# Mixed bands of the first convolution one band later, the upper parts of plain bands copied on ScalarE

## The chip, the cores and the metric

One core of a Trainium2 chip. The metric is the device time of one execution in microseconds (us); a kernel's time is the median of its runs. The profile of one execution shows the engines TensorE (PE, with its weight loads as PEld), VectorE (DVE), ScalarE (ACT), GpSimd (POOL) and SyncE (SP, which issues transfers).

## The reference

The input x is 4 images of 128 channels, 64 by 64, in fp32. Two layers follow each other:

```python
# layer 0: attention over the 4096 positions of an image, 4 heads of 32
x = x + proj(softmax(q @ k.T * scale) @ v)        # q, k, v from a group norm of x
# layer 1: two 3x3 convolutions with quantized weights
out = conv3x3(x, lsq_quantize(w1, alpha1))
out = relu(batchnorm(out, gamma1, beta1))
out = conv3x3(out, lsq_quantize(w2, alpha2))
out = relu(batchnorm(out, gamma2, beta2) + x)
```

The batch norms take mean and variance over all images and positions of a channel. So the first convolution must be complete before the second can start, and the second before the output. The change lies in the two convolutions, which are called the first and the second layer below.

## The kernel before, in words

The order of the instructions on each engine is written out by hand: what the Python code emits first for an engine stands first in its queue. Attention takes up to about 2233 us of the span. It writes its result to `y0` in device memory, and the convolutions read it from there.

A convolution works in 16 bands of 16 rows, four to an image (`bandlist`; band m is image m // 4, rows 16 * (m % 4) on). A band is loaded with a row of margin on each side as a tile `t` of 128 x 18 x 66 (1188 elements a partition). Its fp32 values are split into an upper part, written in the type fp32r, and a lower part, the rest, also in fp32r; both are multiplied by the same weights.

**A plain band** (`split` at L570, `conv` at L803) has `hi`, a copy of `t` (L573), and `lo = t - hi` (L574). TensorE does 9 taps x 2 parts x 2 halves = 36 matmuls of 512 columns (L810) into a PSUM tile of two banks. Each half is then read by VectorE for the statistics (`bn_stats`, L924) and by ScalarE, which copies it to `cv` (L925).

**A mixed band** (`mixed` at L585, `conv_by_two` at L849, `rows_of_two` at L860) computes two rows at a time from sums and differences of rows, with two thirds of the matmuls. VectorE makes `vo` (L591) and the two halves of `vi` (L593, L594); ScalarE copies them to the upper parts `uo` and `ui` (L602); VectorE subtracts for the lower parts `lo` and `li` (L604). TensorE does 24 matmuls (L856) with mixed weights `wmix` (made by `mix_weights`, L840) and the outer taps, into four banks: two in `a`, two in `c`. ScalarE copies one result (L864), VectorE combines all four with four operations (L865 to L868) and takes two statistics (L915).

Which bands are mixed is `BY_TWO` (L583), a set for each layer. PSUM has three two-bank buffers (`pss`, tag "s") and two one-bank buffers (`psa`, tag "a"). The `a` of a mixed band is a `pss` buffer; its `c` is in turn another `pss` buffer or both `psa` buffers (L905). The last band, 15, is plain and uses the two `psa` buffers, one for each half. The band tiles share nine SBUF buffers in `kpool`; the lower parts and `ui` of mixed bands have six more, `upper`.

`layer` (L895) goes over the bands: first band m's matmuls, then `prepare(m)`, which readies band m + 2, then the reading of band m's results. In the first layer `prepare` is `first` (L949): it issues the load of band m + 3 (`load_band`, L608), and splits band m + 2 (`split_band`, L613). It also does three things at fixed bands: `count_bad` (a count that decides at the end whether a general version runs: two small VectorE operations, `big` and `bad`, a matmul `nbad` into a `psa` buffer, and a VectorE copy to `cnt`), the load of the second layer's weights `raw_w` and their copy to `wq[1]`, and `mix_weights(1)` at band 14. Bands 0 and 1 are split while attention ends, and their matmuls and the split of band 2 are interleaved with its last block.

In the second layer `prepare` is `second`, which calls `relu_band` (L977). For a plain band it calls `relu_rows` (L966): ScalarE writes `t` as Relu of the normalized `cv` (L970), then come `hi` (L973) and `lo` (L974). For a mixed band ScalarE's Relu is L981. The first band of the second layer has its own code (L999, L1002).

Of the kernel before, what the change touches and what calls it, by code (L numbers as in the profile page):

```python
# [78 lines left out]
def _fast_body(ctx, tc, x, norm_w, norm_b, qkv_wt, qkv_b, proj_wt, proj_b,  # L79
               w1, alpha1, gamma1, beta1, w2, alpha2, gamma2, beta2, out, cnt):  # L80
    nc = tc.nc
# [142 lines left out]
    def stack_tile(name):  # L224
        return kpool.tile([P, KW], F32R, name=name, tag="k")

    def f32(t):
        return t.bitcast(F32)
# [77 lines left out]
    def keep_warm(count):  # L306

        t = psa.tile([P, FB], F32, name=f"idle{count}", tag="a")
        for _ in range(count):
            nc.tensor.matmul(t[:, 0:P], gavg, gavg, start=True, stop=True)  # L310
# [244 lines left out]
    def band_tile(name):  # L555
        return stack_tile(name).rearrange("p (r w) -> p r w", w=PW)
# [10 lines left out]
        lo, hi = max(r0, 0), min(r1, H)  # L567
        return f32(t)[:, lo - r0 : hi - r0, 1 : 1 + W], lo, hi

    def split(t, name):  # L570

        hi, lo = band_tile(f"hi{name}"), band_tile(f"lo{name}")
        nc.vector.tensor_copy(hi, f32(t))  # L573
        nc.vector.tensor_tensor(lo, f32(t), f32(hi), ALU.subtract)  # L574
        return hi, lo

    raw, ready = {}, {}
    bandlist = [(b, g) for b in range(B) for g in range(H // BR)]
# [1 line left out]

    BY_TWO = (set((3, 5, 7, 9, 11, 13)), set((2, 4, 6, 8, 10, 12, 14)))  # L583

    def mixed(t, name):  # L585

# [24 lines left out]
        nc.sync.dma_start(out=inner, in_=y0[b].rearrange("p (h w) -> p h w", w=W)[:, lo:hi, :])  # L611

    def split_band(b, g):  # L613
        way = mixed if bandlist.index((b, g)) in BY_TWO[0] else split
        ready[0, b, g] = way(raw[b, g], f"0_{b}_{g}")


# [185 lines left out]
    def conv(parts, ps, j, w):  # L803
        hi, lo = parts
        r0 = j * RB
        n = 0
        for part in (hi, lo):
            for tap in range(TAPS):
                kh, kw = divmod(tap, 3)
                nc.tensor.matmul(ps.rearrange("p (r w) -> p r w", w=W), w[:, tap, :],  # L810
                                 part[:, r0 + kh : r0 + kh + RB, kw : kw + W],
                                 start=(n == 0), stop=(n == 2 * TAPS - 1))
                n += 1

    def conv_tile(i, b, g):
        return pss.tile([P, 2, FB], F32, name=f"c{i}_{b}_{g}", tag="s")
# [32 lines left out]
    def conv_by_two(parts, a, c, i):  # L849

        for m, ps, w in ((1, a[0], wmix[:, 0, :, :]), (2, a[1], wmix[:, 1, :, :]),
                         (0, c[0], wq[i][:, 0:3, :]), (3, c[1], wq[i][:, 6:9, :])):
            n = 0
            for part in parts:
                for kw in range(3):
                    nc.tensor.matmul(ps.rearrange("p (r w) -> p r w", w=W), w[:, kw, :],  # L856
                                     part[m][:, :, kw : kw + W], start=(n == 0), stop=(n == 5))
                    n += 1

    def rows_of_two(a, c, y):  # L860

        even, odd = (y.rearrange("p (r e w) -> p r e w", e=2, w=W)[:, :, e, :] for e in range(2))
        a0, a1, c0, c1 = (u.rearrange("p (r w) -> p r w", w=W) for u in (*a, *c))
        nc.scalar.copy(odd, a1)  # L864
        nc.vector.tensor_tensor(even, odd, a0, ALU.add)  # L865
        nc.vector.tensor_tensor(odd, a0, odd, ALU.subtract)
        nc.vector.tensor_tensor(even, even, c0, ALU.add)
        nc.vector.tensor_tensor(odd, odd, c1, ALU.subtract)  # L868
# [11 lines left out]
    def batch_norm(i, st):  # L880

        mv = small.tile([P, 2], F32, name=f"bmv{i}", tag="mv")
        nc.vector.bn_aggr(mv, st)
        r = small.tile([P, 1], F32, name=f"br{i}", tag="rs")
        nc.vector.tensor_scalar(r, mv[:, 1:2], a_q[i], EPS, ALU.mult, ALU.add)
        nc.gpsimd.tensor_tensor(r, r, mhalf, ALU.pow)
        na = small.tile([P, 1], F32, name=f"bn{i}", tag="dv")
        nc.vector.tensor_tensor(na, r, a_n[i], ALU.mult)
        c = small.tile([P, 1], F32, name=f"bc{i}", tag="gc")
        nc.vector.scalar_tensor_tensor(c, mv[:, 0:1], na, bn[i][1], ALU.mult, ALU.add)  # L890
        a = small.tile([P, 1], F32, name=f"ba{i}", tag="ga")
        nc.vector.tensor_tensor(a, r, a_g[i], ALU.mult)
        return a, c

    def layer(i, prepare, done):  # L895


        st = mid.tile([P, B * NB, 6], F32, name=f"st{i}")
        end = mid.tile([P, 15], F32, name=f"end{i}")
        nc.gpsimd.memset(end[:, 0:1], float((B * NB - 2) * FB))  # L900
        for m, (b, g) in enumerate(bandlist[:-1]):
            if m in BY_TWO[i]:
                a = conv_tile(i, b, g)
                a = [a[:, j, :] for j in range(2)]
                if sorted(BY_TWO[i]).index(m) % 2:  # L905
                    c = [psa.tile([P, FB], F32, name=f"c{i}_{b}_{g}{j}", tag="a") for j in "xy"]
                else:
                    c = pss.tile([P, 2, FB], F32, name=f"c{i}_{b}_{g}z", tag="s")
                    c = [c[:, j, :] for j in range(2)]
                conv_by_two(ready[i, b, g], a, c, i)  # L910
                prepare(m)
                y = cv[b][:, 2 * g * FB : (2 * g + 2) * FB]
                rows_of_two(a, c, y)
                for j in range(2):
                    nc.vector.bn_stats(st[:, b * NB + 2 * g + j, :], y[:, j * FB : (j + 1) * FB])  # L915
                continue
            ps = done[m] if m < len(done) else conv_tile(i, b, g)
            for j in range(2):
                if m >= len(done):
                    conv(ready[i, b, g], ps[:, j, :], j, wq[i])  # L920
            prepare(m)
            for j in range(2):
                c = 2 * g + j
                nc.vector.bn_stats(st[:, b * NB + c, :], ps[:, j, :])  # L924
                nc.scalar.copy(cv[b][:, c * FB : (c + 1) * FB], ps[:, j, :])  # L925
        nc.vector.bn_aggr(end[:, 1:3], st.rearrange("p j s -> p (j s)")[:, : 6 * B * NB - 12])
        nc.vector.tensor_scalar(end[:, 2:3], end[:, 2:3], float((B * NB - 2) * FB), None, ALU.mult)
        b, g = bandlist[-1]
        for j in range(2):
            ps = psa.tile([P, FB], F32, name=f"c{i}_last{j}", tag="a")  # L930
            conv(ready[i, b, g], ps, j, wq[i])
            c = 2 * g + j
            nc.vector.bn_stats(end[:, 3 + 6 * j : 9 + 6 * j], ps)
            nc.scalar.copy(cv[b][:, c * FB : (c + 1) * FB], ps)
        prepare(len(bandlist) - 1)
        keep_warm(10)
        return batch_norm(i, end)

    def count_bad():

        big = small.tile([P, 1], F32, name="big")
        nc.vector.tensor_reduce(big, worst, AX.X, ALU.max)
        bad = small.tile([P, 1], F32, name="bad")
        nc.vector.tensor_scalar(bad, big, LIMIT, None, ALU.is_gt)
        nbad = psa.tile([P, FB], F32, name="nbad", tag="a")
        nc.tensor.matmul(nbad[0:1, 0:1], bad, ones[:, 0:1], start=True, stop=True)
        nc.vector.tensor_copy(cnt, nbad[0:1, 0:1])

    def first(m):  # L949
        if m == 4:  # L950
            count_bad()
        if m == 5:
            raw["w"] = f32(stack_tile("raw_w"))[:, : TAPS * P].rearrange("p (t o) -> p t o", o=P)
            nc.sync.dma_start(out=raw["w"], in_=wqd)
        if m == 6:
            nc.vector.tensor_copy(wq[1], raw["w"])
        if m == 14:
            mix_weights(1)
        if 0 < m < len(bandlist) - 3:
            load_band(*bandlist[m + 3])  # L960
        if m + 2 < len(bandlist) and m > 0:
            split_band(*bandlist[m + 2])
# [3 lines left out]
    def relu_rows(b, g, t, r0, r1):  # L966

        inner, lo, hi = t["inner"]
        a, e = max(r0 + g * BR - 1, lo), min(r1 + g * BR - 1, hi)
        nc.scalar.activation(inner[:, a - lo : e - lo, :],  # L970
                             cv[b].rearrange("p (h w) -> p h w", w=W)[:, a:e, :], AF.Relu,
                             bias=c1, scale=a1)
        nc.vector.tensor_copy(t["hi"][:, r0:r1, :], f32(t["t"])[:, r0:r1, :])  # L973
        nc.vector.tensor_tensor(t["lo"][:, r0:r1, :], f32(t["t"])[:, r0:r1, :],  # L974
                                f32(t["hi"])[:, r0:r1, :], ALU.subtract)

    def relu_band(b, g, pieces=((0, BR + 2),)):  # L977
        if bandlist.index((b, g)) in BY_TWO[1]:
            t = band_tile(f"t1_{b}_{g}")
# [13 lines left out]
    t = {n: band_tile(f"{n}1_{b0}_{g0}") for n in ("t", "hi", "lo")}  # L993
# [503 lines left out]
```

## Time and profile before

| what | value |
|---|---|
| median of 3 runs | 2516.44 us (2516.35 to 2517.39) |
| profiled execution | 2515.98 us, its span 2514.1 us |
| TensorE busy in the span | 2472.6 us (98%) |
| VectorE, ScalarE, GpSimd busy | 2205.4, 2106.9, 283.1 us |

By stage, in us from the start of the span:

| stretch | us | PE busy | DVE busy | ACT busy |
|---|---|---|---|---|
| attention, 0 to 2233 | 2233 | 2224.4 | 1994.2 | 2009.8 |
| bands 0 to 2, 2233 to 2262 | 29 | 29.0 | 16.2 | 2.1 |
| bands 3 to 14, 2262 to 2354 | 92 | 88.3 | 78.0 | 24.4 |
| band 15 and statistics, 2354 to 2366 | 12 | 10.9 | 4.8 | 3.1 |
| second layer, 2366 to 2484 | 118 | 117.7 | 91.3 | 49.2 |
| output, 2484 to 2514.1 | 30.1 | 2.3 | 20.9 | 18.4 |

A line of the timeline has the start in us, the time taken in us, the engine, the line of the kernel, the operation, the tile written, "<-" and the tiles read, the shapes, and how many instructions are merged; in brackets stands the idle time before it and what ended that. In the groups, the two numbers after the bar are busy us in all and the mean of one in ns, and the next is the engine's idle time just before them. PEclk is the share of the full TensorE clock that was granted.

### The profile page before, as it was taken

Reading aid. Unit: us, or ns where it says so; the run is one execution under the profiler, and the core shown is the slowest. Engines: PE = TensorE matmul, PEld = TensorE weight load, DVE = VectorE, ACT = ScalarE, POOL = GpSimd, SP = SyncE. Lnnn points to the kernel's source line nnn. Section 1 sums busy time; section 2 is a strip of 40 time slices with the busy share of each in tenths; the row PEclk is TensorE's granted clock in tenths of the full one; section 3 lists DMA queues with packets and bytes.
Section 4 is the critical chain, followed back from the end, with each engine's and each line's share of the span. In section 5 each row is a group of like instructions: output and inputs, shape, how many; then the busy total and the mean of one; then the engine's idle time right before and its main releaser. Section 6 shows DMA issues by size and latency. Waiting matters only on the chain.

```text
span 2514.1 us, 64863 instructions
## 1 busy us (share of the span) xinstructions
PE 2472.6 (98%) x28552; PEld 1474.0 (59%) x28552; DVE 2205.4 (88%) x1501; ACT 2106.9 (84%) x2291; POOL 283.1 (11%) x461
## 2 busy tenths in 40 slices
PE   9999999999999999999999999999999999999995
PEld 6555555555555555555555555555555555567774
DVE  6899888899988988889988889879999999978687
ACT  5999888999988899999988999989999999952344
POOL 2111111111011111111111111110001000100000
PEclk9999999999999999999999999999999999999998
DMA  6877677788766676788757666797666666664304
GB/s 194 191 184 170 167 177 171 175 197 190 182 156 166 171 173 152 169 213 189 168 141 184 177 148 167 172 216 174 139 143 147 143 134 152 135 131 94 109 1 168
DMA packets 148953, 403.84 MB, mean 161 GB/s; under 512 B 59416, under 2 KB 60184, under 8 KB 120120
## 3 DMA queue, kind: packets, MB, share of 16 engines
q0 software_dynamic: 45840, 280.39, 48.8%
q1 hardware_dynamic: 100952, 113.60, 17.1%
q8 instruction: 226, 3.70, 0.6%
q10 hardware_dynamic: 1872, 5.64, 0.6%
q14 instruction: 63, 0.52, 0.1%
HBM read 107.48 MB, written 56.42 MB: 65 GB/s over the span
## 4 chain that ended last, share of the span: by engine, by line
PE 87%; DMA 4%; issue 4%; DVE 3%; ACT 1%; SPq 1%; ACTq 0%; POOL 0%; POOLq 0%; DVEq 0%
PE s L442 40%; PE acc L456 36%; PE c L810 4%; DMA rm<-p 2%; DVE r L471 1%; DMA rc<-rd 1%; PE l L488 1%; PE pk L317 1%; PE pq L317 1%; PE c L856 1%; PE pv L317 1%; PE po L317 1%; DMA q<-qd 1%; SPq L422 0%; PE c_2z L856 0%
## 5 line engine op out<-in xcount | busy, mean ns | idle before, releaser
L444 ACT ACTIVATE p<-s 128x1024 f32<-128x1024 f32 x2048 | 1950.6, 1032 | 200.1 <-PE s L442 154.2
L471 DVE TENSOR_TENSOR r<-r,p 128x2048 f32<-128x2048 f32 x768 | 1758.0, 2289 | 64.3 <-ACT p L444 13.9
L442 PE MATMUL s<-q,k 64*128 64x512 f32 x8192 | 1138.3, 409 | 1.1 <-ACT p L444 0.9
L456 PE MATMUL acc<-p,v 128*32 128x256 f32 x16384 | 1026.4, 383 | 0.0
L442 PEld LDWEIGHTS s<-q,k 64*128 64x128 f32 x8192 | 715.7, 184 | 409.2 <-issue 165.8
L456 PEld LDWEIGHTS acc<-p,v 128*32 128x32 f32 x16384 | 462.5, 109 | 483.6 <-issue 248.1
L466 POOL DMA_DIRECT2D rm<-p x160 | 139.6, 873 | 796.5 <-ACT p L444 591.1
L925 ACT COPY cv<-c 128x512 f32<-128x512 f32 x34 | 20.0, 587 | 130.3 <-DVE st L924 130.3
L352 DVE SCALAR_TENSOR_TENSOR kst<-pk,b,kst 128x512 fp32r<-128x512 f32 x32 | 24.0, 750 | 83.5 <-PE s L442 68.5
L469 DVE TENSOR_TENSOR r<-p,p 128x2048 f32<-128x2048 f32 x32 | 73.2, 2288 | 11.1 <-ACT p L444 11.0
L810 PE MATMUL c<-hi,wq 128*128 128x512 f32 x306 | 79.1, 402 | 2.1 <-ACT hi L999 1.4
L810 PE MATMUL c<-lo,wq 128*128 128x512 f32 x306 | 78.5, 400 | 0.0
L352 DVE SCALAR_TENSOR_TENSOR qst<-pq,b,qst 128x512 fp32r<-128x512 f32 x32 | 24.0, 751 | 58.3 <-PE s L442 47.3
L810 PEld LDWEIGHTS c<-hi,wq 128*128 128x128 f32 x306 | 57.2, 188 | 19.7 <-issue 3.6
L810 PEld LDWEIGHTS c<-lo,wq 128*128 128x128 f32 x306 | 57.6, 188 | 15.4
L356 POOL DMA_DIRECT2D qd<-qst x31 | 23.6, 762 | 267.0 <-DVE qst L352 223.0
L492 POOL DMA_DIRECT2D r<-rm x31 | 26.2, 845 | 219.0 <-DMA rm<-p 87.5
L924 DVE BATCH_NORM_STATS2 st<-c 128x6 f32<-128x512 f32 x34 | 23.7, 696 | 20.0 <-ACT cv L925 11.2
L356 POOL DMA_DIRECT2D kd<-kst x27 | 20.0, 742 | 178.1 <-DVE kst L352 169.4
L488 PE MATMUL l<-r,ones 128*32 128x256 f32 (+1 forms) x504 | 37.7, 382 | 0.0
L351 ACT ACTIVATE kst<-pk,b 128x512 fp32r<-128x512 f32 x32 | 22.3, 700 | 18.3 <-PE pk L317 18.3
L464 POOL DMA_DIRECT2D rm<-p x32 | 17.9, 559 | 175.1 <-ACT p L444 84.3
(200 smaller groups left out, 1022.4 us busy)
## 6 DMA issues: line engine op xcount, KB each, us to landing
rm<-p POOLq DMA_DIRECT2D x192, 1024.0 KB, 7.9
q<-qd SPq DMA_DIRECT2D x248, 128.0 KB
r<-rm POOLq DMA_DIRECT2D x31, 1024.0 KB, 7.6
x<-in_x_dram SPq DMA_DIRECT2D x86, 256.0 KB
k<-kd SPq DMA_DIRECT2D x124, 128.0 KB
qd<-qst POOLq DMA_DIRECT2D x31, 512.0 KB, 5.2
kd<-kst POOLq DMA_DIRECT2D x27, 512.0 KB, 4.8
y<-x POOLq DMA_DIRECT2D x32, 256.0 KB, 6.4
```

Of the source, the lines that this page charges most:

```text
L317: nc.tensor.matmul(out[cs, :], w[:, cs], x, start=True, stop=True)
L352: nc.vector.scalar_tensor_tensor(lo, ps[what], bias, t[:, 0, :], ALU.add, ALU.subtract)
L356: (nc.sync if start else nc.gpsimd).dma_start(out=dst[b, j].rearrange("s p n -> p s n"), in_=t)
L442: nc.tensor.matmul(s[:, i, :], k[r, half, c0 : c0 + P], q[r, half, part, :], start=(part == 0), stop=(part == 1))
L444: nc.scalar.activation(pts[step][:, 2 * half : 2 * half + 2, :], s, AF.Exp, scale=SCALE)
L456: nc.tensor.matmul(acc[n][h * D : (h + 1) * D, cs], v[:, kt % KB, h * D : (h + 1) * D], pt[:, h, cs], start=(kt == 0 and half == 0), stop= ...
L466: nc.gpsimd.dma_start(out=msum[n], in_=pt, accum_op=ALU.add)
L469: nc.vector.tensor_tensor(rsum[n], pts[step - 1], pt, ALU.add)
L471: nc.vector.tensor_tensor(rsum[n], rsum[n], pt, ALU.add)
L488: nc.tensor.matmul(t["l"][h * D : (h + 1) * D, cs], ones, r[:, h, cs], start=first, stop=end)
L492: nc.gpsimd.dma_start(out=rsum[n], in_=msum[n], accum_op=ALU.add)
L810: nc.tensor.matmul(ps.rearrange("p (r w) -> p r w", w=W), w[:, tap, :], part[:, r0 + kh : r0 + kh + RB, kw : kw + W], start=(n == 0), stop ...
```

## The change

The mixed bands of the first layer move from 3, 5, ..., 13 to 4, 6, ..., 14; there are six of them still. In the first layer the upper part `hi` of the plain bands from 3 on is copied by ScalarE in place of VectorE; the second layer's `relu_rows` does the same. The choice of PSUM buffers for a mixed band's `c` is counted back from the last mixed band, which gets a `pss` buffer: in the first layer bands 14, 10 and 6 have `pss`, bands 12, 8 and 4 the two `psa` buffers; in the second layer each band keeps what it had. `count_bad` moves from band 4 to band 5.

```diff
-    def split(t, name):
+    def split(t, name, beside=True):
 
         hi, lo = band_tile(f"hi{name}"), band_tile(f"lo{name}")
-        nc.vector.tensor_copy(hi, f32(t))
+        if beside:
+            nc.vector.tensor_copy(hi, f32(t))
+        else:
+            nc.scalar.copy(hi, f32(t))
         nc.vector.tensor_tensor(lo, f32(t), f32(hi), ALU.subtract)
         return hi, lo
...
-    BY_TWO = (set((3, 5, 7, 9, 11, 13)), set((2, 4, 6, 8, 10, 12, 14)))
+    BY_TWO = (set((4, 6, 8, 10, 12, 14)), set((2, 4, 6, 8, 10, 12, 14)))
...
     def split_band(b, g):
-        way = mixed if bandlist.index((b, g)) in BY_TWO[0] else split
+        m = bandlist.index((b, g))
+        way = mixed if m in BY_TWO[0] else lambda t, name: split(t, name, m < 3)
         ready[0, b, g] = way(raw[b, g], f"0_{b}_{g}")
...
-                if sorted(BY_TWO[i]).index(m) % 2:
+                if (max(BY_TWO[i]) - m) % 4:
                     c = [psa.tile([P, FB], F32, name=f"c{i}_{b}_{g}{j}", tag="a") for j in "xy"]
                 else:
                     c = pss.tile([P, 2, FB], F32, name=f"c{i}_{b}_{g}z", tag="s")
...
     def first(m):
-        if m == 4:
+        if m == 5:
             count_bad()
...
-        nc.vector.tensor_copy(t["hi"][:, r0:r1, :], f32(t["t"])[:, r0:r1, :])
+        nc.scalar.copy(t["hi"][:, r0:r1, :], f32(t["t"])[:, r0:r1, :])
```

## The prediction

> **What bounds the kernel now.** I read the page first, then the chain of waits that ended last, then TensorE's waits stage by stage.
>
> ```profile
> span 2514.1 us, 64863 instructions
> ...
> PE 2472.6 (98%) x28552; PEld 1474.0 (59%) x28552; DVE 2205.4 (88%) x1501; ACT 2106.9 (84%) x2291; POOL 283.1 (11%) x461
> ```
>
> TensorE (PE) is busy for 98% of the span, so only its idle time and slow time can be won. The change touches the two convolution layers alone: bands 0 to 2 of the first layer keep their old way, so attention, up to 2233 us, issues what it did. TensorE's waits from 2259 to 2364 us (first layer from band 2 on) and from 2366 to 2484 us (second layer) are these, with columns waiter, releaser, total, times and longest:
>
> ```profile
> PE c L856 <- ACT ui L602: 3.0, 1, 3.0
> PE c L810 <- ACT cv L925: 0.7, 1, 0.7
> ```
> ```profile
> PE c L810 <- ACT hi L999: 1.4, 1, 1.4
> ```
>
> The second layer waits once, for its first tile, which the change leaves as it is. The first layer waits twice, and TensorE's timeline shows where:
>
> ```profile
> 2259.91 2.31 PE L810 MATMUL c<-lo,wq 128*128 128x512 f32 x9
> 2265.20 1.65 PE L856 MATMUL c<-ui,wmix 128*128 128x512 f32 x3 [2.98 <-ACT ui L602]
> 2266.64 1.49 PE L856 MATMUL c<-li,wmix 128*128 128x512 f32 x3
> 2267.94 0.98 PE L856 MATMUL c<-ui,wmix 128*128 128x512 f32 x3
> ...
> 2273.21 0.99 PE L810 MATMUL c<-hi,wq 128*128 128x512 f32 x3 [0.72 <-ACT cv L925]
> ```
>
> Band 2 ends at 2262.22. Band 3, the first mixed one, waits 2.98 us for its parts; its first six matmuls then take 2.74 us (2265.20 to 2267.94), where later in the band six take 1.44 (2269.47 to 2270.91). The table by stretch gives the reason in its PEclk column (third from the right):
>
> ```profile
> 2265.00:2268.00 3.00, 2.80 (x7) 2.05 (x8) 2.35 (x4) 0.73 (x2) 0.00 (x0) 0.50 0.43 79
> ...
> 2366.20:2369.00 2.80, 2.71 (x11) 2.18 (x12) 1.49 (x2) 2.80 (x4) 0.00 (x0) 1.00 0.00 0
> ```
>
> After the wait of 2.98 us the granted clock is 0.50; after the 1.36 us at the second layer's start it is 1.00.
>
> From 2262.22 to the last band's start at 2353.94 are 91.72 us. Steady work is 8.60 us for a plain band (2287.97 to 2296.57) and 5.75 for a mixed one (2296.57 to 2302.32); six of each are 86.1. So 5.6 us are lost here: 2.98 and 0.72 of waits, 1.3 to 1.5 of half clock, and restarts of about 0.15 (band 4 takes 8.77). **5.6 us is the most that the first layer can give.**
>
> [...] 2.98 us did it, 0.72 and 1.36 did not. [...] The groups by shape agree (0.77 us against 1.40 at 1188 elements):
>
> ```profile
> L573 DVE CAST hi<-t 128x1188 fp32r<-128x1188 f32 x7 | 5.4, 767 | 0.0
> L574 DVE TENSOR_TENSOR lo<-t,hi 128x1188 fp32r<-128x1188 f32 x7 | 9.8, 1396 | 0.3
> L602 ACT CAST uo<-vo 128x1056 fp32r<-128x1056 f32 x13 | 14.0, 1077 | 14.3 <-DVE vo L591 14.3
> L925 ACT COPY cv<-c 128x512 f32<-128x512 f32 x34 | 20.0, 587 | 130.3 <-DVE st L924 130.3
> ```
>
> So the copy leaves the engine that does it faster. [...] The trace shows st, cv, st, cv strictly in turn, 1.35 us from one st to the next.
>
> **The change part by part.** *The copy on ScalarE.* No row has 1188 elements. From L925 and L602 the slope is 0.9 ns per element, so 1.20 us, an estimate[...]. Bounds: 1.08 (L602, fewer elements) and 1.40 (the Relu L970, 1353 ns for 1152, scaled). I take 1.20. Fifteen copies leave VectorE (seven bands of layer one, eight of layer two, 0.77 each, 11.5 us), 18 us go to ScalarE, which has 24.4 busy in the first layer's 92 us. None is on TensorE's path but where written below.
>
> *Band 3 plain, band 4 mixed.* Step by step from VectorE's st at 2259.51, whose start the change leaves alone. ScalarE's second cv ends at 2262.22; the copy hi3 is next in its queue and runs 2262.12 to 2263.32 (successors start 0.1 early in the trace). TensorE starts band 3 at **2263.38**: a wait of 1.16 in place of 2.98, and at full clock. Behind the copy, VectorE waits with lo3 until 2263.35 (done 2264.75, needed 2265.6); behind lo3 are band 1's two st (2264.66, 2266.01), then band 4's split at 2266.62. That split takes 4.84 from vo to the next st (2261.51 to 2266.35 now), so its parts are ready by 2271.5. Band 3 ends 2263.38 + 8.77 = 2272.15, and **band 4 starts without a wait**. Its PSUM is the buffer of band 1, free at 2267.3. Ends: band 4 2277.90; band 5 (parts ready 2276.7, buffer of band 2 free 2274.1) 2286.50.
>
> *count_bad one band later.* It adds nothing (one matmul, three small VectorE operations, no DMA) but moves behind rows_of_two of band 4, and its matmul stands in TensorE's queue ahead of band 6. Today it is in time by half a microsecond (TensorE reaches it at 2281.98):
>
> ```profile
> 2281.28 0.15 DVE L944 TENSOR_SCALAR bad<-big 128x1 f32<-128x1 f32 x1
> 2282.21 0.15 DVE L947 CAST cnt<-nbad 1x1 int32<-1x1 f32 x1 [0.77 <-PE nbad L946]
> ```
>
> Afterwards: band 2's st at 2271.46 and 2272.81, its cv until 2274.13, hi5 until 2275.23, lo5 2275.26, band 3's st 2276.57 and 2277.92, band 6's split 2278.53, rows_of_two(4) +4.81 = 2283.34, big +3.83 = 2287.17, bad done 2287.5, the matmul at about 2287.65. TensorE has been there since 2286.50: **a new wait of 1.15 us**, with band 6 queued behind it. Band 6 starts near 2287.85. SP reads cnt too (its load at 2282.4 stands before raw_w at 2283.43); this moves to 2288, and should raw_w and band 8's load stay behind it they land by 2294.5, vo8 runs then and its parts exist at 2298.1, for a start at 2302.2: nothing.
>
> *The rest of the first layer.* VectorE now needs 4.81 + 3.83 + 1.31 + 1.96 = 11.9 us per pair of bands, TensorE 14.35; hi runs ahead on an idle ScalarE. Five mixed and four plain bands, 28.75 + 34.4, put the last band at **2351.0** instead of 2353.94.
>
> *Band 14 mixed.* mix_weights(1) must now wait for band 14's first twelve matmuls (2.9 us into 5.75), then rows_of_two and the statistics end 9 us after band 14's start; the last band's first half ends at 10.05. Hidden. With its outer sums in the two-bank buffers, both psa buffers are free for the last band since band 12; without that it would wait for rows_of_two(14). The reordered parity leaves the second layer's buffers as they are.
>
> *Second layer.* TensorE waits nowhere there. hi1 delays the second band's t by 1.2 us, VectorE's lo1 and vo2 by 0.3, against a start of band 2 at 2383.74 with parts ready at 2376.7. VectorE's period falls from 14.75 to 13.95. Worth 0. Were hi not early, the period would be 15.2, 0.9 over TensorE's, for six pairs 5.3 us, inside the 7 us of lead. The end of the layer and the output are unchanged.
>
> *Sum.* Won: 1.82 of the first wait, 0.72 of the second, about 1.5 of half clock and restart; lost: 1.15 and a restart of 0.15. Net 2.94 us. The span goes from 2514.1 to 2511.2; 1.9 lie around it (the profiled execution took 2515.98); the median of the runs, 2516.44, stands 0.46 above that execution. So **2513.5**. What a measurement can tell from no change is about 0.2%, 5.0 us: this is within it.
>
> **The rivals.** *In time at count_bad:* if bad is 1.15 us earlier, the gain is 4.2, 2512.2. Against it: the chain is a sum of 20 measured durations; for it: two hand-overs might be shorter. *No waits at all:* 5.6 us, 2510.8. It needs hi3 at 2262.2, but the copy stands behind cv. *The wait that replaces the one removed, slower than before:* VectorE's chain (two copies on ScalarE, each waited for) reaches bad 1.6 us later than I say. Then TensorE stands 2.75 us at count_bad, the clock halves as it did at 2265, and the loss there is 2.75 + 1.5 against 1.3 reckoned: gain 0, 2516.5; each further microsecond costs one. It decides from a wait near 2.75 us; the copy at its upper bound adds only 0.4. *The change does not do what it says:* band 3 could still wait for band 0's cv buffer; that ends at 2262.2, so hardly; gain below 1, 2516.
>
> **How the numbers follow.** Forecast 0.59; in time 0.19; no waits 0.10; replaced wait 0.09; no effect 0.03. Faster by over 0.2% means below 2511.4, the no-wait case: 0.10. Within: 0.87. Slower by over 0.2% needs four more microseconds in the replaced wait: 0.03. The range 2511.3 to 2516.2 takes in the copy's bounds (0.2 less to 0.4 more), 1 us for the spread of runs (2516.35 to 2517.39), and leaves out the two outer cases.
>
> **What would show it.** TensorE waiting about 1.2 us for hi at band 3, none at band 4, about 1.1 at nbad with clock 1.00 throughout; hi on ACT at 1.2 us; c_last near 2351. A wait at nbad over 2.5 us, or any new wait in the second layer, would prove the sum wrong.

## The result and the profile after

The changed kernel takes 2511.93 us in the median (2510.75 to 2515.09, 20 runs), the kernel before 2516.39 (2513.78 to 2519.04, 20 runs): a ratio of 0.9982 with a 95% interval of 0.9976 to 0.9989. That is 4.5 us less, with 2.8 to 6.0 by the interval: small, but clear of no change. The forecast was 2513.5, 2.9 us less, and no difference that clears 0.2%.

The profiled execution spans 2511.1 us (2514.1 before). The head of the page and TensorE's waits from 2255 us to the end (waiter, releaser, total, times, longest):

```profile
span 2511.1 us, 64860 instructions
...
PE 2471.6 (98%) x28552; PEld 1473.1 (59%) x28552; DVE 2194.6 (87%) x1486; ACT 2123.7 (85%) x2306; POOL 281.6 (11%) x461
```
```profile
PE c L814 <- ACT hi L1003: 1.3, 1, 1.3
PE nbad L950 <- DVE bad L948: 1.0, 1, 1.0
PE c L814 <- ACT hi L576: 0.3, 1, 0.3
```

VectorE lost 10.8 us and ScalarE gained 16.8, near the 11.5 and 18 reckoned. The wait of 2.98 us for a mixed band's parts and the one of 0.72 for a buffer are gone. Two others stand there: 0.3 us for the ScalarE copy of band 3, and 1.0 us at count_bad. The third is the second layer's start, as before. TensorE's timeline, and two rows of the table by stretch with the granted clock (third figure from the right):

```profile
2260.27 2.31 PE L814 MATMUL c<-lo,wq 128*128 128x512 f32 x9
2262.90 2.42 PE L814 MATMUL c<-hi,wq 128*128 128x512 f32 x9 [0.32 <-ACT hi L576]
...
2271.60 0.87 PE L860 MATMUL c<-ui,wmix 128*128 128x512 f32 x3
...
2287.09 0.19 PE L950 MATMUL nbad<-ones,bad 128*1 128x1 f32 x2 [1.02 <-DVE bad L948]
...
2350.43 2.31 PE L814 MATMUL c_last<-hi,wq 128*128 128x512 f32 x9
```
```profile
2262.00:2266.00 4.00, 3.68 (x16) 2.62 (x15) 2.41 (x3) 1.44 (x2) 0.17 (x2) 1.00 0.64 140
2286.00:2290.00 4.00, 2.98 (x15) 2.31 (x15) 3.08 (x7) 0.51 (x1) 0.00 (x0) 1.00 0.48 98
```

Band 2 ends at 2262.58 (the start of its last matmuls and the time that they take), band 4 starts at 2271.60 without a wait, the last band at 2350.43. The clock is full behind both waits. **From the end of band 2 to the last band's start are now 87.85 us; they were 91.72.** This stretch is the measure of all that follows. It is read inside one execution of each kernel, while attention ahead of it ends up to 3.5 us earlier or later from one execution to the next (its last projection starts between 2250.1 and 2253.6 us in the ten profiles here), which blurs differences of a microsecond in the times. How well it repeats can be seen at band 3: five kernels have the same instructions up to there, and wait 0.32 or 0.33 us.

The wait at count_bad is the end of a chain that runs through the moved copies. The chain that ended last, in order of time, for this stretch:

```profile
2261.66 1.20 ACT hi L576
...
2262.88 1.40 DVE lo L577
...
2273.56 1.20 ACT hi L576
...
2274.79 1.40 DVE lo L577
...
2286.88 0.17 DVE bad L948
...
2287.09 0.19 PE nbad L950 x2
```

Twice the chain goes to ScalarE for a copy and back to VectorE for the lower part; only behind nbad does TensorE set the pace.

### The profile page after: what moved, and what is told of

It is laid out like the page before. It is cut to its first block, busy times and chain, and to the rows that moved or that the text cites. A ratio compares the mean times of both kernels' runs of the same rounds, so it can differ in the third digit from the quotient of the medians.

```text
span 2511.1 us, 64860 instructions
## 1 busy us (share of the span) xinstructions
PE 2471.6 (98%) x28552; PEld 1473.1 (59%) x28552; DVE 2194.6 (87%) x1486; ACT 2123.7 (85%) x2306; POOL 281.6 (11%) x461
## 4 chain that ended last, share of the span: by engine, by line
PE 89%; issue 4%; DMA 3%; DVE 2%; ACT 1%; POOL 0%; ACTq 0%; SPq 0%; POOLq 0%; DVEq 0%
PE s L442 41%; PE acc L456 37%; PE c L814 3%; DMA rm<-p 3%; PE l L488 1%; PE pq L317 1%; PE c L860 1%; PE po L317 1%; PE pv L317 1%; PE pk L317 1%; DVE r L471 1%; PE c_2z L860 1%; ACT res L1039 0%; ACT p L444 0%; PE c_last L814 0%
```

## The experiments

Stretch and times are in one table; the edits follow, with what was left out marked by dots. "Start of layer two" is from the end of band 2 to the second layer's first matmul. The kernel before had a median of 2516.39 us beside the changed kernel and of 2515.95 beside sets_only, copies_only, count_late and early_three, so ratios are compared here, not medians. The last four rest on one execution each.

| kernel | stretch, us | start of layer two, us | ratio to before, interval |
|---|---|---|---|
| before | 91.72 | 104.07 | 1 |
| changed | 87.85 | 100.11 | 0.9982, 0.9976 to 0.9989 |
| sets_only | 86.15 | 98.43 | 0.9975, 0.9965 to 0.9985 |
| copies_only | 92.52 | 104.75 | 1.0010, 1.0003 to 1.0016 |
| count_late | 86.72 | 99.01 | 0.9985, 0.9978 to 0.9992 |
| early_three | 86.03 | 98.30 | 0.9980, 0.9971 to 0.9988 |
| parity_old | 88.90 | 101.22 | one run |
| before_load5 | 90.89 | 103.22 | one run |
| count_slow1 | 89.13 | 101.43 | one run |
| count_slow2 | 91.87 | 104.17 | one run |

**The order of the bands without the copies (sets_only).** From the changed kernel:

```diff
-        way = mixed if m in BY_TWO[0] else lambda t, name: split(t, name, m < 3)
+        way = mixed if m in BY_TWO[0] else lambda t, name: split(t, name)
...
-        nc.scalar.copy(t["hi"][:, r0:r1, :], f32(t["t"])[:, r0:r1, :])
+        nc.vector.tensor_copy(t["hi"][:, r0:r1, :], f32(t["t"])[:, r0:r1, :])
```

> The bands, PSUM buffers and count_bad of the changed kernel, but every copy of hi on VectorE as before. My theory, that the gain comes from the order of the bands and that the copies on ScalarE cost a little at the start: from the end of band 2 to the last band's start about 86.7 us (91.7 before, 87.9 changed), a wait of 0 to 0.2 us at band 3, 0 to 0.3 us at nbad, none in the second layer, total about 1 us below the changed kernel. The rival, that the relief of VectorE makes the gain: VectorE stays late, waits of over 1 us remain at band 3 or nbad or come at a later band, stretch 89 us or more, total above the changed kernel.

TensorE's waits from 2245 us on:

```profile
PE c L814 <- ACT hi L1003: 1.3, 1, 1.3
```

No wait is left in the first layer, and the stretch is 86.15 us, 1.70 below the changed kernel. VectorE, with the copies back on it, is not too late for anything. The new order of the bands, with the buffers and the place of count_bad that came with it, is worth 5.57 us, all that the prediction called possible (5.6).

**The copies without the order (copies_only).** The kernel before, with the copies alone (`split` gets its argument `beside`):

```diff
-        way = mixed if bandlist.index((b, g)) in BY_TWO[0] else split
+        m = bandlist.index((b, g))
+        way = mixed if m in BY_TWO[0] else lambda t, name: split(t, name, m < 3)
...
-        nc.vector.tensor_copy(t["hi"][:, r0:r1, :], f32(t["t"])[:, r0:r1, :])
+        nc.scalar.copy(t["hi"][:, r0:r1, :], f32(t["t"])[:, r0:r1, :])
```

> The bands, PSUM buffers and count_bad of the kernel before, with the copies of hi on ScalarE from band 3 on and in the second layer. My theory: the wait of 2.98 us at band 3 and the half clock after it stay, band 4 waits about 1.7 us instead of 0.7 since VectorE waits for hi4, stretch from band 2 to the last band about 92.6 us, total 0.5 to 1 us above before. The rival, that the relief of VectorE makes the gain: stretch 90 us or less, total 2 to 3 us below before.

TensorE's waits from 2245 us on:

```profile
PE c L860 <- ACT ui L605: 2.9, 1, 2.9
PE c L814 <- ACT cv L929: 1.3, 1, 1.3
PE c L814 <- ACT hi L1003: 1.2, 1, 1.2
```

Band 3's wait stays, band 4's grows from 0.72 to 1.28, the stretch is 92.52 where 92.6 was expected, and the times are slower beyond their interval. So the copies on ScalarE cost 0.8 us of the stretch with the old order and 1.7 with the new one. The rival that they make the gain is refuted. The median is 2.5 us slower (0.8 to 4.0 by the interval), more than the stretch accounts for. The rest stays open: in this profile the output took 1.8 us longer than before, but its length differs by as much among the ten profiles (30.1 to 31.9 us).

**count_bad later (count_late).** The changed kernel with one number changed:

```diff
-        if m == 5:
+        if m == 9:
             count_bad()
```

> The changed kernel with count_bad at band 9 instead of 5. My theory: the wait at nbad goes and nothing takes its place, stretch about 86.7 us, total about 1.1 us below the changed kernel. The rival: VectorE is as late as before, and TensorE waits the same 1 us for the parts or buffers of band 6 or 8, stretch 87.9 us, total as changed.

TensorE's waits from 2245 us on:

```profile
PE c L814 <- ACT hi L1003: 1.3, 1, 1.3
PE c L814 <- ACT hi L576: 0.3, 1, 0.3
```

The wait goes and none takes its place: 86.72 us, 1.13 less. The times do not show it (a ratio of 0.9985 against 0.9982): a microsecond is below what they resolve.

**Band 3 split early (early_three).** From sets_only, with count_bad at band 9:

```diff
     last["sums_at_once"]()
+    split_band(*bandlist[3])
...
-        if m + 2 < len(bandlist) and m > 0:
+        if m + 2 < len(bandlist) and m > 1:
             split_band(*bandlist[m + 2])
```

> As the kernel with every hi copy on VectorE and the mixed bands one later, count_bad at band 9, and band 3 split on VectorE while it idles at the end of attention, before the last store of attention. My theory: no wait from band 2 to the last band, stretch 86.2 us, total 1.5 to 2 us below the changed kernel, about 2510.2. The rival: the split delays the last block's store on VectorE, and with it the mixed weights and band 0's reading, by up to 2 us, and a wait comes back at band 4: stretch 87.5 us or more, total as changed.

The stretch is 86.03, only 0.12 below sets_only, which had no waits either. So about 86.0 is the floor, twelve bands of steady work. Both versions have lower ratios than the changed kernel, but the intervals overlap: that they are better is shown by the stretch alone.

**The old choice of buffers (parity_old).** The changed kernel with one line as before:

```diff
-                if (max(BY_TWO[i]) - m) % 4:
+                if sorted(BY_TWO[i]).index(m) % 2:
```

> The changed kernel with the old choice of PSUM buffers: band 14 then has both one-bank buffers, which the last band needs. My theory, from the changed kernel's profile, where VectorE reads band 14's third result until 0.9 us after the last band's start: TensorE waits about 0.9 us at the last band's first half, not at its second, and the stretch from band 2 to the second layer's start grows by 0.9 us. The rival: the wait is taken up by the statistics behind it, and the second layer starts when it did.

TensorE's waits from 2255 us to the second layer's start:

```profile
PE c L814 <- ACT cv L929: 1.3, 1, 1.3
PE c_last L814 <- DVE cv L871: 0.4, 1, 0.4
PE c L814 <- ACT hi L576: 0.3, 1, 0.3
```

The new choice is worth 1.05 us, but half of my expectation failed. At the last band it saves a wait of 0.4 us and not of 0.9. The rest is at band 5: with the old choice band 4 took a third two-bank buffer, so band 5 waited 1.3 us for ScalarE to have read band 3, and the wait at nbad, 1.0 in the changed kernel, was gone, since TensorE came later. From the end of band 2 to nbad the two together make 0.50 us (25.01 against 24.51). The wait at the last band was not taken up behind it: the second layer starts 1.1 us later too.

**What moved VectorE's first reading (before_load5).** The kernel before, with one load moved:

```diff
+        if m == 3:
+            load_band(*bandlist[5])
-        if 0 < m < len(bandlist) - 3:
+        if 0 < m < len(bandlist) - 3 and m != 2:
             load_band(*bandlist[m + 3])
```

> The kernel before, with only the load of band 5 moved behind the one of band 3's turn, to about 2262 us. My theory, that this load shares the way with attention's last store in the kernel before and not in the changed one: the mixed weights wait 0.4 us for the store instead of 1.2, VectorE's first reading of band 0 comes 0.8 us earlier against TensorE, and the wait at band 3 is about 2.2 us instead of 2.98. If the clock halves only after a longer wait, the half clock is gone as well and the stretch from band 2 to the last band is about 89.5 us, else about 91. The rival, that the store's time is chance: the wait for it stays at 1.2 us, band 3 waits 2.9 to 3.0, stretch 91.7.

In the changed kernel the load of band 5 takes the SBUF buffer of hi1, which comes free before that of lo1, which it took before. SP's timeline shows its issue, before and changed; then VectorE's wait for the store of attention's last block, before and changed:

```profile
2252.48 0.36 SPq L611 DMA_DIRECT2D t<-y  x1
```
```profile
2250.68 0.36 SPq L614 DMA_DIRECT2D t<-y  x1
```
```profile
DVE wmix L847 <- DMA y<-x: 1.2, 1, 1.2
```
```profile
DVE wmix L851 <- DMA y<-x: 0.4, 1, 0.4
```

With the load moved away in the kernel before, that wait is 0.4 us as well, band 3 waits 2.15, and the stretch is 90.89, 0.83 less: with the load under way the store landed about 0.8 us later. The other profiles agree: the wait is 1.2 us in the two kernels with the old order and this load early, and 0.4 in the eight others. The half clock stayed, though, as TensorE's timeline shows:

```profile
2262.88 0.98 PE L856 MATMUL c<-ui,wmix 128*128 128x512 f32 x3 [2.15 <-ACT ui L602]
2264.18 1.23 PE L856 MATMUL c<-li,wmix 128*128 128x512 f32 x3 [0.31 <-DVE li L604]
2265.20 1.48 PE L856 MATMUL c<-ui,wmix 128*128 128x512 f32 x3
```

The first three matmuls after the wait run at full pace; then TensorE waits once more, 0.31 us for li, and the next matmuls are slow (1.48 us for three in place of 0.98). The last section has what the records of the clock show of it.

**A longer wait at count_bad (count_slow1, count_slow2).** The changed kernel with one needless reduction, or with two (`range(2)`, count_slow2):

```diff
+        for _ in range(1):
+            nc.vector.tensor_reduce(big, cv[0][:, :2 * FB], AX.X, ALU.max)
         nc.vector.tensor_reduce(big, worst, AX.X, ALU.max)
```

> The changed kernel with one needless VectorE reduction of 1024 elements (about 1.25 us) ahead of count_bad, to see what a longer wait of TensorE costs. My theory: the wait at nbad is 2.2 to 2.3 us instead of 1.02, the clock stays at full rate, the stretch grows by 1.25 us to 89.1. The rival, that any wait over about 1.4 us halves the clock: stretch 90.5 us, granted clock 0.5 for some 3 us behind the wait.

> As the kernel with one needless reduction ahead of count_bad, with two. My theory: the wait at nbad is 3.5 us, the clock halves behind it for about 3 us as at band 3 in the kernel before, the stretch grows by 2.5 us of wait and 1.4 of slow matmuls, to about 91.8. The rival, that the half clock at band 3 had another cause than the wait: full clock, stretch 90.4 us.

The waits are 2.28 and 3.54 us, the stretches 89.13 and 91.87 (89.1 and 91.8 expected). The stretch behind the wait, first of count_slow1, then of count_slow2; PEclk is the third figure from the right:

```profile
2287.80:2291.00 3.20, 3.20 (x15) 2.56 (x16) 2.30 (x4) 0.59 (x1) 0.00 (x0) 1.00 0.00 0
```
```profile
2287.00:2291.00 4.00, 4.00 (x12) 3.14 (x13) 3.08 (x5) 0.85 (x2) 0.00 (x0) 0.58 0.00 0
```

The longer wait is paid once as a wait and again as slow matmuls.

## Why the prediction was right, and where it was not

**The copy's price.** 1.20 us was taken for it. In the groups by shape:

```profile
L977 ACT CAST hi<-t 128x1188 fp32r<-128x1188 f32 x8 | 9.5, 1187 | 0.7
...
L576 ACT CAST hi<-t 128x1188 fp32r<-128x1188 f32 x7 | 8.3, 1188 | 0.0
```

1.19 us; the slope of two rows gave 1.20.

**Band 3 plain.** Right in kind: a short wait for hi3 at full clock, none at band 4. Mis-sized: 1.16 us expected, 0.32 measured. The step that failed is "whose start the change leaves alone": VectorE's st was to come 2.71 us ahead of band 2's end (2259.51 against 2262.22) and comes 3.51 ahead (2259.07 against 2262.58); before, then changed:

```profile
2259.51 0.69 DVE L924 BATCH_NORM_STATS2 st<-c 128x6 f32<-128x512 f32 x1
```
```profile
2259.07 0.69 DVE L928 BATCH_NORM_STATS2 st<-c 128x6 f32<-128x512 f32 x1
```

I followed the buffers for releases but not for the moment at which a load starts, and so missed that band 5's load leaves the store's way. before_load5 shows what that load does by itself, in the kernel before. The shorter wait is 0.84 of the 0.93 us by which the stretch came out shorter than forecast (88.78).

**count_bad.** Right: 1.15 us forecast. Band 5 starts at 2277.32; reckoned with 8.60 us of work, as the forecast did, it is done 1.17 us ahead of nbad at 2287.09, and the profile counts 1.02 as waiting. count_late shows that the wait is paid in full (1.13 us). The prediction booked this wait to the later place of count_bad. sets_only has the same place and no wait: the copies put VectorE behind there. Twice VectorE hands the copy to ScalarE and waits 1.7 us for it:

```profile
DVE lo L577 <- ACT hi L576: 3.5, 2, 1.7
```

Less the 0.8 saved on each, that is 1.9 us; from VectorE's first st to bad are 27.81 us in the changed kernel (2259.07 to 2286.88) and 25.79 in sets_only (2259.52 to 2285.31). The prediction had both hand-overs in its chain but never set the order without the copies beside it. So the copies got no price of their own in it, when they take 1.7 of the 5.6 us.

**The rest of the first layer, band 14, the second layer.** Right. From nbad's start at 2287.09 to the last band are 63.34 us; 63.15 were reckoned as work, and 0.1 is the matmul itself. The second layer lasts 117.73 us before, 117.65 changed and 117.68 in sets_only: the copies there are worth nothing. Of the new choice of buffers the prediction named the use at the last band and not the one at band 5, which is worth about as much (0.50 us net of the 1.05).

**The sum.** 2.94 us forecast, 3.87 in the stretch. The forecast is the difference of two starts of the last band (2353.94 and 2351.0); the terms listed for it add up to 2.74 only, so "about 1.5" for half clock and restart should have been 1.7. The profiled span agrees almost exactly with its forecast of 2511.2, but by luck: attention ended 0.36 us later and the output took some 0.7 longer than in the profile before, which hid the larger gain. The median fell by 4.46 us, and up to the second layer's start the profiles account for 3.96 of it (104.07 less 100.11); the 0.5 left over is well inside the interval.

**The rivals.** In time at count_bad and no waits at all exist as kernels, count_late and sets_only, but not as this change. The replaced wait did occur and was as short as forecast; count_slow2 shows its price: at a wait of 3.5 us the stretch is 91.87, and the gain is gone. Its point of decision, 2.75 us for a lost gain, stood too low, since the gain was larger than reckoned; that a wait of 2.75 us halves the clock was an estimate, which no run tried (behind 2.28 us it stayed at 1.00, behind 2.98 it was 0.50). That band 3 waits for another buffer did not occur: its wait is for hi.

## What to carry to other kernels

Follow the chain, not the busy share: a copy moved to an idle engine still costs its hand-over where the receiving engine waits for it at once (here twice 1.7 us of wait on VectorE, 1.7 us of the stretch), and it was free where it ran ahead, in the second layer (117.65 us with the copies, 117.68 without). Price each part of a change alone as well as in the sum, because a part with a cost hides behind one with a gain. When the order of tiles in a rotating pool changes, check for every load when its new buffer comes free and what else is under way then: here a load issued at 2252.48 us made a store land about 0.8 us later.

## What the runs showed of the hardware

The length of a wait does not alone tell whether TensorE's clock is halved behind it. Behind a wait of 2.28 us (count_slow1) the granted clock stayed at 1.00; behind waits of 2.93 (copies_only), 2.98 (before) and 3.54 us (count_slow2) the matmuls were slow, three of them taking up to 1.65, 1.65 and 1.48 us against 0.87 to 0.89 later in the band, and so they were behind one of 2.15 us with a second of 0.31 behind it (before_load5, up to 1.48 us).

The records of the clock tell more. In the kernel before, the clock is 0.50 from 2264.76 to 2268.17 us, for 3.413 us, and then 1.00 for 221.87 us, to the drop after the last matmuls at 2490.03: 65 times as long. Here are stretches of this length, laid end to end from a change of the clock in the same profile: the one that holds most of TensorE's wait and the one behind it, of before, of before_load5 and of count_slow1. The figure behind the comma is TensorE's busy time; PEclk is the third from the right:

```profile
2261.34:2264.76 3.42, 0.88 (x4) 0.37 (x2) 3.42 (x5) 2.35 (x3) 0.17 (x2) 1.00 0.38 87
2264.76:2268.17 3.41, 2.97 (x7) 2.22 (x8) 2.76 (x4) 0.97 (x2) 0.00 (x0) 0.50 0.47 90
```
```profile
2261.33:2264.74 3.41, 1.54 (x5) 0.97 (x6) 3.40 (x4) 1.35 (x2) 0.00 (x0) 1.00 1.31 224
2264.74:2268.16 3.42, 3.42 (x9) 2.64 (x8) 2.74 (x4) 1.17 (x2) 0.00 (x0) 0.50 0.14 23
```
```profile
2286.10:2289.51 3.41, 1.74 (x9) 1.40 (x10) 3.06 (x7) 0.00 (x0) 0.00 (x0) 1.00 0.35 60
2289.51:2292.92 3.41, 3.41 (x16) 2.67 (x15) 2.70 (x4) 1.17 (x2) 0.18 (x2) 1.00 0.00 0
```

Behind 0.88 and 1.54 us of work in such a stretch the clock was 0.50 in the next; behind 1.74 us it was 1.00. The wait of count_slow1 lies in two of them: 0.61 us of it fell into the one before. In the kernel before, a stretch with 1.62 us of work in attention (1691.32 to 1694.73) has the full clock behind it as well:

```profile
1691.32:1694.73 3.41, 1.62 (x24) 0.30 (x14) 1.66 (x2) 1.25 (x2) 0.00 (x0) 1.00 1.08 236
1694.73:1698.14 3.41, 3.41 (x42) 2.02 (x40) 3.31 (x2) 2.55 (x3) 0.00 (x0) 1.00 0.99 221
```

Up to the end of the second layer every other stretch of before has at least 2.05 us of work, every one of the changed kernel at least 2.12; the clock is full behind all of them. That the work in such a stretch decides, and not the wait as a whole, is an estimate from these few figures (0.88, 1.54, 1.62, 1.74); whether a line lies between 1.54 and 1.62 is not shown.

In count_slow2 the slow matmuls cost 1.5 us: its stretch is 2.74 us over that of count_slow1, and 1.26 of these are wait.
